# Two groups of every eight transposed wholly by blocks, with a sum, the routing and a product moved in the order

## The chip, the cores and the metric

The kernel runs on one core of one Trainium2 chip. The metric is the device time of one execution in microseconds, as the median of several runs. A profile of one execution shows the engines: TensorE (PE, with its weight loads as PEld), VectorE (DVE), ScalarE (ACT), GpSimd (POOL) and SyncE (SP), which issues DMAs.

## What is computed

A decoder layer on x of 16 sequences of 256 tokens with 256 channels, all in float32: three blocks, each followed by a layer norm over the residual.

```
x = layernorm(x + attn(x));  x = layernorm(x + xattn(x, ctx, frac));  x = layernorm(x + ffn(x))

attn:   scores = q k^T (k, v from weights, 4 heads of 64);  p = relu(scores)^2;  residual + p v
xattn:  16 heads of 16;  logits = Q K^T * scale
        D = clip(frac_k - frac_q, -0.2, 0.2)
        probs = softmax(gamma * logits + delta * (ap_h * max(D,0) + an_h * min(D,0)))
        out = (probs V) Wo^T + bo
ffn:    top1 = argmax(gate(x));  base = x wi^T + wi_b
        inter = relu(base + lora_B[top1] lora_A[top1] x);  out = inter wo^T + wo_b
```

## The kernel before

The first block (attn) comes first, in a loop over eight blocks of 512 rows. The change does not touch it. After it runs one loop over `n = 0 ... 65`, which holds the cross attention and nearly all of the ffn. The order of all instructions on every engine's queue is the order in which this loop writes them; there is no scheduler behind it.

**Groups.** One step of the loop is one group: four heads of one sequence, and there are 4 x 16 = 64 groups. In step n the names `now`, `nxt`, `last` and `older` are the groups n, n + 1, n - 1 and n - 2. For one group:

- `negative` (L642, GpSimd) writes the negative part of the bias into a tile `neg` of which there are three; `positive(g)` (L654, ScalarE) writes the positive part into PSUM bank g.
- `logits` (L664, PE, 32 small matmuls) adds the products into the four banks.
- `maxima` (L682, VectorE, eight instructions with one accumulator read each) adds bank and `neg`, writes the result over `neg`, and keeps the maximum of each row.
- Then the probabilities have to be transposed, so that keys lie on partitions. In the way of PE, `subtract` (L733) takes the maximum off, `turned(g)` (L743) transposes four 128x128 tiles per head into PSUM, and `exps(g)` (L750, ScalarE) takes the exponential on the way to `pT`.
- From group 14 to 61 a group is *direct*: heads 0 and 1 go by blocks instead. `exp_rows` (L696, ScalarE) takes the exponential in rows, `blocks` (L707, VectorE) transposes 32x32 blocks into a tile of its own (`z` for even groups, the tile `kT`, free by then, for odd ones) and writes it to DRAM (L712); `fetch` (L724) reads it back with four DMAs into the right rows of `pT`. Heads 2 and 3 keep the way through PE.
- `attend` (L764, PE) multiplies `pT` with the values into a bank `ps_v`; `keep` (L777) copies it out, every second group.

**Parts.** From n = 15 on, eight steps carry one block of 512 rows through the ffn; `part` is (n - 15) % 8, and there are six such cycles in the loop (cycle 31 to 38 is the third). Part 0 transposes the rows (L857), part 1 forms the gates (L872), part 2 and 3 are the `halved` steps: in part 2 `route` (L887 to L909) picks the expert, `turn_um` (L919) transposes the result, and in both `inner` (L945) computes four of the eight tiles of hidden units into the same four PSUM banks that the logits use, `lora` (L958) adds the low-rank part, and ScalarE and VectorE write relu of it to `hT` (L967, L971). Parts 4 to 7 form the last product, one quarter of the rows each: `finish(j)` is `outer` (L978, PE) and `add` (L991, VectorE: sum with the rows, then statistics). Parts 5 and 7 put it into a `ps_v` bank, so that `attend` of two groups comes one step later, together (`apart`). In part 3 the block before it is scaled and sent out (`done.ready`, L208 to L215 and L1006).

**The PSUM tiles** `ps_b` are used in a ring of three (`tile_b`), by transposes and products alike. SyncE's queue is in order: an issue that waits holds those behind it. The DMAs of the loop on it are those named, the fetch and write of values and sums (`gather`, `regroup`, `invert`, `spread`, L574 to L600), the loads of the next sequence (L444, L448) and the output.

**What stood in a whole cycle's order.** In the two halved steps `turned` and `exps` of the last group's heads 2 and 3 came directly after the maxima and ahead of `inner`; in all other direct steps they came at the end of the step. `blocks` of a group was written in its own step, except in parts 0 and 1, where it was written after the maxima of the next step (`later`). Its fetch came at the start of the next step, or at the end of it for `later`.

Of the kernel before, what the change touches and what calls it, by code (L numbers as in the profile page):

```python
# [9 lines left out]
FP = mybir.dt.float32  # L10
AF = mybir.ActivationFunctionType
ALU = mybir.AluOpType
# [10 lines left out]
def tile_decoder_layer(ctx: ExitStack, tc: tile.TileContext, a: dict, out: bass.AP):  # L23
# [403 lines left out]
    if True:  # L427
# [199 lines left out]
        class Group:  # L627
            def __init__(self, batch, og):
                self.batch = batch
                self.o, self.i = divmod(og, 2)  # L630
                self.direct = DIRECT <= 4 * batch.b + og < 4 * B - 2
# [43 lines left out]
            def maxima(self):  # L675
# [3 lines left out]
                for g in range(4):  # L679
                    minus = self.direct and g < 2  # L680
# [12 lines left out]
            def exp_rows(self, g):  # L693

                for j in range(2):
                    nc.scalar.activation(  # L696
                        self.t[:, g, j, :], self.t[:, g, j, :], AF.Exp,
                        bias=self.mx[:, g, j : j + 1], scale=-1.0,
                    )

            def blocks(self):

                if self.i:
                    self.z = kT.rearrange("p n (c h q) -> p n c h q", c=2, q=32)
                else:
                    self.z = pm.tile([P, 4, 2, 4, 32], FP, tag="z", bufs=1, name="z")
                nc.vector.transpose(  # L707
                    self.z.rearrange("p n c h q -> p h c n q"),
                    self.t[:, 0:2].rearrange("p g j (c n k) -> p (g j) c n k", c=2, k=32),
                )  # L710
                self.away = drams.tile([P, 4, 4 * P // 2], FP, tag="blocks", name="away_z")
                nc.sync.dma_start(  # L712
                    out=self.away, in_=self.z.rearrange("p n c h q -> p n (c h q)")
                )

            def room(self):
# [3 lines left out]
                self.pD = self.pT[:, 0:2].rearrange("p g (a c h q) -> p (g a) c h q", a=2, c=2, q=64)  # L720

            def fetch(self):
                for n in range(4):
                    nc.sync.dma_start(  # L724
                        out=self.pT[32 * n : 32 * n + 32, 0:2].rearrange("k g (a e) -> k (g a) e", a=2),
                        in_=self.away[:, n].rearrange("(r k) e -> k r e", k=32),
                    )

            def subtract(self, halves):
                for g, eng in ((2, nc.gpsimd),) if self.direct else zip((0, 2), halves):  # L730
# [21 lines left out]
            def attend(self):  # L752
# [4 lines left out]
                for k in range(2):  # L757
                    for g in range(4):
                        rhs = self.pT[:, g, k * S : (k + 1) * S]
                        to = batch.av[32 * g : 32 * g + 32, self.i * S : (self.i + 1) * S]  # L760
                        if self.direct and g < 2:
                            rhs = self.pD[:, :, k, g, :].rearrange("p r (j q) -> p j r q", j=2)
# [20 lines left out]
        MADE, DIRECT = 5, 14  # L783
# [649 lines left out]
```

## Time and profile before

| | us |
|---|---|
| median of 3 runs | 887.77 (887.74 to 887.83) |
| the profiled execution | 887.49 |
| its span in the profile | 885.7 |
| VectorE: maxima L682, 512 instructions of 420 ns | 181.5 |
| PE: transposes L743, 640 | 87.1 |
| PE: last product L978, 512 | 115.6 |
| VectorE: block transposes L707, 48 of 1.24 us | 59.6 |
| ScalarE: exponentials in rows L696, 192 of 498 ns | 81.3 |
| ScalarE: pT from PSUM L750, 160 of 590 ns | 87.4 |
| GpSimd: subtractions L733, 65 of 1.91 us | 124.0 |

In the page's first part each engine has its busy time, its share of the span, and its number of instructions. The granted TensorE clock is at 9 of 10 or more in all forty slices of the span. A line of a timeline gives the start in the span, the time until the last of the instructions it merges had ended, the engine, the source line, and how many there are; in square brackets stands the time for which the engine was idle before it and what ended that. In a view of waits the three numbers are the total, how often, and the longest. A line such as "ps_v<-pT,vaug" reads: written tile, then the tiles read.

### The profile page before, as it was taken

The numbers are of one execution on the slowest core, as the hardware profiler recorded it, in microseconds if no ns is written. First come the engines' busy times: TensorE is split into PE (matmuls) and PEld (weight loads), VectorE is DVE, ScalarE is ACT, GpSimd is POOL, SyncE is SP. The second block draws the span as 40 slices with busy tenths as digits, with TensorE's granted clock in tenths as the row PEclk, the third lists the DMA queues.
The fourth block names the chain that finished last, engine by engine and source line by source line (L and its number), as shares of the span: only waits on it lengthen the run. The fifth ranks groups of instructions, "written<-read, shape, count | busy, mean of one in ns | idle before, by whom it ended". The sixth has DMA issues, their size and how long they took to land.

```text
span 885.7 us, 20853 instructions
## 1 busy us (share of the span) xinstructions
PE 862.4 (97%) x7708; PEld 513.1 (58%) x7708; DVE 693.3 (78%) x1975; ACT 577.0 (65%) x1012; POOL 466.6 (53%) x455
## 2 busy tenths in 40 slices
PE   8999999999999999999999999999999999999997
PEld 4334444444456776567547656754765675576655
DVE  6878899889779898769778877877887787777444
ACT  5766777777788788647747765774875577475111
POOL 1100223322479898656828765883976678374010
PEclk9999999999999999999999999999999999999999
DMA  5501101010001333454454536445453644642001
GB/s 139 159 1 43 54 24 44 31 49 1 8 8 48 99 98 110 139 162 149 158 155 150 158 129 184 151 155 168 138 164 133 193 151 135 181 149 102 28 7 41
DMA packets 70373, 92.94 MB, mean 105 GB/s; under 512 B 13824, under 2 KB 55296, under 8 KB 70272
## 3 DMA queue, kind: packets, MB, share of 16 engines
q1 hardware_dynamic: 69696, 91.35, 33.2%
q8 instruction: 61, 1.00, 0.5%
q14 instruction: 40, 0.33, 0.1%
q10 hardware_dynamic: 576, 0.26, 0.1%
HBM read 50.43 MB, written 39.58 MB: 102 GB/s over the span
## 4 chain that ended last, share of the span: by engine, by line
PE 44%; DVE 11%; issue 2%; POOL 1%; ACT 1%; DMA 0%; ACTq 0%; POOLq 0%; DVEq 0%
PE ps_l L945 9%; PE ps_b L978 6%; PE ps_l L664 5%; PE ps_v L764 5%; PE ps_b L743 4%; DVE neg L682 3%; PE ps_b L614 3%; PE ps_v L978 3%; PE ps_b L477 2%; PE ps_l L958 2%; DVE z L707 1%; PE ps_b L503 1%; PE ps_b L532 1%; POOL neg L733 1%; DVE dpos L547 1%
## 5 line engine op out<-in xcount | busy, mean ns | idle before, releaser
L682 DVE CUSTOM_DVE_ANT_0 neg<-ps_l,neg 128x256 f32<-128x256 f32 x512 | 181.5, 420 | 41.4 <-PE ps_l L664 38.3
L642 POOL TENSOR_SCALAR neg<-dneg,aneg,delta 128x512 f32<-128x512 f32 x252 | 198.9, 804 | 20.9 <-PE ps_b L743 10.0
L654 ACT ACTIVATE ps_l<-dpos,apos_d 128x512 f32<-128x512 f32 x256 | 172.2, 688 | 49.9 <-DVE mx L682 30.9
L354 DVE TENSOR_TENSOR pr<-pr 128x1024 f32<-128x1024 f32 x128 | 153.8, 1243 | 30.2 <-ACT pr L353 29.8
L733 POOL TENSOR_TENSOR neg<-neg,mx 128x1024 f32<-128x1024 f32 x65 | 124.0, 1909 | 85.4 <-DVE mx L682 84.3
L353 ACT ACTIVATE pr<-ps_a 128x1024 f32<-128x1024 f32 x128 | 125.0, 1026 | 53.0 <-PE ps_a L345 52.7
L345 PE MATMUL ps_a<-xnT,kT 64*64 64x512 f32 x1024 | 124.6, 593 | 1.0 <-ACT xnT L330 0.4
L364 PE MATMUL ps_v<-pr,vv 64*64 64x512 f32 x1024 | 122.7, 589 | 0.0
L945 PE MATMUL ps_l<-xt,wi 128*128 128x512 f32 x248 | 111.7, 596 | 0.2
L750 ACT ACTIVATE pT<-ps_b 128x512 f32<-128x512 f32 x160 | 87.4, 590 | 32.4 <-PE ps_b L743 30.9
L743 PE MATMUL ps_b<-ident,neg 128*128 128x128 f32 x640 | 87.1, 277 | 3.4 <-ACT pT L750 2.3
L743 PEld LDWEIGHTS ps_b<-ident,neg 128*128 128x128 f32 x640 | 71.5, 141 | 24.0 <-issue 6.2
L364 PEld LDWEIGHTS ps_v<-pr,vv 64*64 64x64 f32 x1024 | 45.0, 133 | 64.5 <-issue 54.6
L379 POOL TENSOR_TENSOR xt<-xt,half 128x512 f32<-128x512 f32 x15 | 19.1, 1274 | 119.8 <-ACT half L378 119.8
L419 POOL TENSOR_TENSOR hid<-hid,bo 128x256 f32<-128x256 f32 x32 | 43.6, 1366 | 71.8 <-ACT hid L251 71.8
L696 ACT ACTIVATE neg<-neg,mx 128x256 f32<-128x256 f32 x192 | 81.3, 498 | 0.0
L764 PE MATMUL ps_v<-pT,vaug 128*32 128x256 f32 x1024 | 74.3, 385 | 7.2 <-DVE x L991 6.0
L664 PE MATMUL ps_l<-kM,qT 32*64 32x256 f32 x2048 | 79.8, 388 | 0.0
L345 PEld LDWEIGHTS ps_a<-xnT,kT 64*64 64x64 f32 x1024 | 41.9, 133 | 65.3 <-issue 52.5
L945 PEld LDWEIGHTS ps_l<-xt,wi 128*128 128x128 f32 x248 | 45.6, 191 | 49.4 <-issue 44.6
L978 PE MATMUL ps_b<-wof,hT 128*128 128x256 f32 x304 | 68.4, 380 | 0.0
L524 POOL TENSOR_SCALAR kM<-keys,of_head 128x512 f32<-128x512 f32 x22 | 38.7, 1760 | 48.4 <-DVE keys L513 48.4
(137 smaller groups left out, 1183.3 us busy)
## 6 DMA issues: line engine op xcount, KB each, us to landing
pT<-away_z SPq DMA_DIRECT2D x192, 128.0 KB
away_z<-z SPq DMA_DIRECT2D x24, 512.0 KB
away_z<-kT SPq DMA_DIRECT2D x24, 512.0 KB
away_v<-raw SPq DMA_DIRECT2D x16, 512.0 KB
cT<-in_ctxT SPq DMA_DIRECT2D x16, 256.0 KB
v<-away_v SPq DMA_DIRECT2D x32, 128.0 KB
invs<-rows SPq DMA_DIRECT2D x16, 256.0 KB
x<-in_x SPq DMA_DIRECT2D x7, 512.0 KB
```

Source lines behind the costliest of these rows:

```text
L345: nc.tensor.matmul(sc[64 * k : 64 * k + 64, h, :], lhsT=kT[64 * h : 64 * h + 64, q, hf * P + 64 * k : hf * P + 64 * k + 64], rhs=self.xnT[ ...
L353: nc.scalar.activation(pr, sc, AF.Relu)
L354: nc.vector.tensor_tensor(pr, pr, pr, ALU.mult)
L364: nc.tensor.matmul(self.acc[k][64 * h : 64 * h + 64, :], lhsT=vv[64 * k : 64 * k + 64, hf, 64 * q : 64 * q + 64], rhs=pr[64 * k : 64 * k + ...
L642: nc.gpsimd.tensor_scalar(self.neg[:, g], self.batch.dneg, aneg[:, h : h + 1], delta, ALU.mult, ALU.mult,)
L654: nc.scalar.activation(banks[g], self.batch.dpos.rearrange("p j k -> p (j k)"), AF.Copy, scale=apos_d[:, h : h + 1],)
L664: nc.tensor.matmul(banks[g][64 * h : 64 * h + 64, j * S : (j + 1) * S], lhsT=self.batch.qT[rows, self.o, j * P + 64 * h : j * P + 64 * h + ...
L682: nc.vector.tensor_tensor_reduce(out=self.t[:, g, j, :], in0=banks[g][:, j * S : (j + 1) * S], in1=self.neg[:, g, j, :], scale=-1.0 if min ...
L733: eng.tensor_tensor(rows, rows, top.to_broadcast([P, 4, S]), ALU.subtract)
L743: nc.tensor.transpose(ps[:, k * S + j * P : k * S + (j + 1) * P], self.t[:, g, j, k * P : (k + 1) * P], ident,)
L945: nc.tensor.matmul(self.banks[g], lhsT=wi[:, c, f * P : (f + 1) * P], rhs=self.xT[:, c, :], start=(c == 0), stop=False,)
L978: nc.tensor.matmul(ps[:, 0:C], lhsT=self.hT[f][:, j * P : (j + 1) * P], rhs=wof[:, f, :], start=(f == 0), stop=(f == FC - 1),)
```

## The change

- A direct group now has a number of `pairs`: 2 where `(n - 15) % 8` is 2 or 3, that is in groups 17, 18, 25, 26, 33, 34, 41, 42, 49, 50, 57 and 58, and 1 in the other direct groups. With two pairs all four heads go by blocks: eight exponentials in rows instead of four, two block transposes instead of one (the first into `z`, the second into `kT`), two writes of 512 KB, and four fetches of 256 KB instead of 128 KB. No subtraction, no `turned` and no `exps` is left for such a group. For every direct group the scratch in DRAM gets a dimension for the pair, so that of a whole group a write goes in rows of 1 KB, not 4 KB, and a fetch in rows of 2 KB, not 1 KB.
- In the halved steps `turned` and `exps` of the last group no longer stand ahead of `inner`; where the last group has one pair (part 2) they stand at the end of the step, as in the other direct steps.
- `later` now holds in part 2 too: the blocks of group 33 are written in step 34, after its maxima, and its fetch directly behind them. For all groups with `later` the fetch moves from the end of that step to directly behind the blocks.
- `route` moves ahead of the blocks of the last group in part 2.
- The first `finish` moves to the start of part 4, ahead of the logits. In parts 5 to 7 `finish` moves ahead of `blocks`.
- In part 3 the scaling of the older block's rows (`done.ready`) moves from VectorE to GpSimd; its three Newton steps stay on VectorE.

```diff
@@ Group @@
-                self.direct = DIRECT <= 4 * batch.b + og < 4 * B - 2
+                n = 4 * batch.b + og
+                self.direct = DIRECT <= n < 4 * B - 2
+                self.pairs = 0
+                if self.direct:
+                    self.pairs = 2 if n > DIRECT and (n - DIRECT - 1) % 8 in WHOLE else 1
...
+                self.away = drams.tile(
+                    [P, 4, self.pairs, 2 * P], FP, tag=f"blocks{self.pairs}", name="away_z"
                 )
+                for m in range(self.pairs):
+                    if m or self.pairs == 1 and self.i:
+                        z = kT.rearrange("p n (c h q) -> p n c h q", c=2, q=32)
+                    else:
+                        z = pm.tile([P, 4, 2, 4, 32], FP, tag="z", bufs=1, name="z")
+                    nc.vector.transpose(
...
+                    nc.sync.dma_start(
+                        out=self.away[:, :, m], in_=z.rearrange("p n c h q -> p n (c h q)")
+                    )
...
-                for g, eng in ((2, nc.gpsimd),) if self.direct else zip((0, 2), halves):
+                for g, eng in ((2, nc.gpsimd),)[: 2 - self.pairs] if self.direct else zip((0, 2), halves):
...
-        MADE, DIRECT = 5, 14
+        MADE, DIRECT, WHOLE = 5, 14, (2, 3)
@@ the loop @@
+            if ff and part == 4:
+                ff.finish(0)
             if now:
                 now.logits()
...
                 now.maxima()
-                now.later = n >= FIRST and part in (0, 1)
+                now.later = n >= FIRST and part in (0, 1, 2)
+            if halved and part == 2:
+                ff.route()
             if last and last.direct and last.later:
                 last.blocks()
+                last.fetch()
...
             if halved:
-                for g in range(2, 4) if last.direct else range(2):
-                    last.turned(g)
-                    last.exps(g)
-                if part == 2:
-                    ff.route()
-                if now.direct:
-                    for g in range(2):
-                        now.exp_rows(g)
+                now.exp_rows()
                 now.subtract((nc.gpsimd, nc.vector))
-                if now.direct:
+                if not now.later:
                     now.blocks()
...
-                    done.ready(newton(done.mv, done.near, 4))
+                    done.ready(newton(done.mv, done.near, 4), eng=nc.gpsimd)
                 ff.inner(part - 2, range(0, 3))
...
+            if ff and part > 4:
+                ff.finish(part - 4, tile_v() if apart else None)
             if now and now.direct and not halved and not now.later:
                 now.blocks()
-            if ff and part >= 4:
-                ff.finish(part - 4, tile_v() if apart else None)
-            if last and (not last.direct or now and now.direct and not halved):
-                for g in range(2, 4):
+            if last and (not last.direct or now and now.direct):
+                for g in range(2 * max(last.pairs, 1), 4):
                     last.turned(g)
                     last.exps(g)
...
-            if last and last.direct and last.later:
-                last.fetch()
```

## The prediction

> **What bounds the kernel now.** I read the page first, then the waits of TensorE, then TensorE's timeline through one cycle of eight groups (31 to 38; the stage of group n begins with its logits, L664), and last VectorE, ScalarE and SyncE beside it.
>
> ```profile
> PE 862.4 (97%) x7708; PEld 513.1 (58%) x7708; DVE 693.3 (78%) x1975; ACT 577.0 (65%) x1012; POOL 466.6 (53%) x455
> ```
>
> PE is busy 97% of 885.7 us, so only what leaves PE's own sequence, or the few waits in it, can shorten the kernel. The waits (us in total, times, longest):
>
> ```profile
> PE ps_v L764 <- DVE x L991: 6.0, 6, 1.6
> PE ps_b L919 <- DVE um L909: 2.6, 5, 0.5
> ...
> PE ps_b L503 <- DVE x L991: 0.7, 1, 0.7
> ...
> PE ps_b L464 <- DVE x L991: 0.2, 1, 0.2
> ```
>
> The last products' sums (L991) hold PE for 6.0 + 0.7 + 0.2 = 6.9 us, the routing (L909) for 2.6. What stands around the transposes that go (start, us, instruction; idle time in brackets):
>
> ```profile
> 449.84 1.60 PE L664 MATMUL ps_l<-kM,qT 32*64 32x256 f32 x32
> 451.37 1.09 PE L743 MATMUL ps_b<-ident,neg 128*128 128x128 f32 x8
> 452.58 7.13 PE L945 MATMUL ps_l<-xt,wi 128*128 128x512 f32 x16
> ```
> ```profile
> 452.10 0.42 DVE L682 CUSTOM_DVE_ANT_0 neg<-ps_l,neg 128x256 f32<-128x256 f32 x1
> ```
>
> That is group 26, one of the new "whole" ones' stages. The inner product L945 overwrites the bank that VectorE's maxima still read: bank 0 needs its two maxima, the second from 452.10 to 452.52. L945 starts at 452.58, though L743 was through at 452.46. So the eight transposes already stand in the shadow of the maxima.
>
> ```profile
> 497.99 1.25 DVE L707 STREAM_TRANSPOSE z<-neg 128x1024 f32<-128x1024 f32 x1
> 499.16 0.38 DVE L991 TENSOR_TENSOR x<-x,ps_v 128x256 f32<-128x256 f32 x1
> ```
> ```profile
> 499.60 2.65 PE L764 MATMUL ps_v<-pT,vaug 128*32 128x256 f32 x32 [1.10 <-DVE x L991]
> ```
>
> Here the sum that frees the bank stands behind a block transpose on VectorE, and PE waits 1.10 us for it.
>
> **Part by part.** Whole are the stages of parts 2 and 3: 17, 18, 25, 26, ... 57, 58, twelve groups in six cycles. My clock is cycle 31 to 38 (33 and 34 whole).
>
> *Sums ahead of block transposes (parts 5 to 7).* The sum then starts 1.17 us earlier (499.16 - 497.99), or earlier still where the transpose itself waited for exponentials (before 786.63 VectorE idled 2.03 us). That exceeds the waits of 0.78 to 1.10; the one of 1.63 (788.23) goes too. Next late is ScalarE: it idles 0.84 us before the copies of L860 at 504.65, and the positives ahead of them follow VectorE, whose summed work is unchanged. So 0.26 of the 1.10 stays. The six: 0.89 + 0.84 + 0.79 + 0.78 + 0.78 + 1.63 = 5.7; with 0.67 and 0.16, **-6.5 us**. Ends: nothing, and -6.9.
>
> *Part 2 (group 33).* Group 32's eight transposes are not removed but put at the stage's end. At their old place PE gains nothing: maxima begin 1.3 us after the logits, L945 still starts about 515.3. Route ahead of z: um comes 1.17 us earlier, so L919's 0.53 us goes. At the end +0.95 us of transposes (479.21 to 480.17), but the logits of 34, which ran 1.53 us instead of 1.05 (527.73 to 529.26 in the chain that ended last) because ScalarE's positives came late, lose that 0.48. 0.95 - 0.53 - 0.48 = **-0.06, taken as 0**. Ends: -0.5 and +0.5 a cycle.
>
> *Part 3 (group 34).* Group 33's transposes go, and the wait for the maxima, about 1.06 us, takes their place: **0**. VectorE now does maxima of 34 (to 532.2), two transposes of 33 (1.24 each, to 534.7), then z of 34. z is one buffer, so this waits until z of 33 has been written away. SyncE writes at about 533.5; the trace has 549.62 to 552.38, 2.76 us, from such an issue until the fetch behind it goes, and SyncE's own waits for these writes are at most 3.4 us elsewhere, 3.7 with the 0.34 of the issue. So z of 34 starts at 536.3, kT of 34 at about 537.7, through at 539. The three Newton steps (0.9) follow, then the hidden units' eviction at 540 instead of 538.53. Queued behind it are keys, dpos, the positives of 35 and the first last product. That product now runs 541.3 to 544.75 ahead of the logits, and covers it: positives of 35 end near 543.
>
> The writes' rows change: 512 of 1 KB for 128 of 4 KB. The fetches move 1 KB rows today with the same engines; I take equal speed. Ends: none, and 1.5 us more per write, the whole transfer again by these rows (packets of about 1.6 us between issue and landing). SyncE sends the fetch of 33 at 537.8, done about 542; its values are needed at 545.8. It also stands ahead of output, rows and the fetch of 34 in SyncE's queue, with needs near 557.
>
> ScalarE trades two pT copies (1.08 together) for four more exponentials (1.7) in each whole stage, inside idle times of 4.48 (before 522.08) and 5.93 us (before 538.49): 0. GpSimd loses two subtractions (1.9 each) a cycle and, in the five cycles with an older output, gains four row scalings: 0.56 us each by L845's row, 2.2 us. VectorE loses 1.38 (534.75, four). A row against it: dpos (L547) took 0.69 us at 528.37 with GpSimd idle, but 1.72 us at 495.40 beside GpSimd's L733 and L524. If it came to that here, 1.04 us of VectorE per cycle, covered by the first last product: 0, ends 0 and +1.0.
>
> [...]
>
> *Part 4 (group 35).* PE before: 541.28 logits (1.53), values 1.0, L532 1.9, first last product 3.45, transposes 0.88, L464 0.5, next logits 550.54. After: product to 544.75, logits 1.05 to 545.8, values 546.8, L532 548.6, L464 549.1. But now little lies between logits and logits. The sum of row 0 (1.0 us) and the maxima of 35 start near 546.0 (543.04 before). ScalarE's positives end 3.65 us after the maxima start (543.04, 546.69 before): 549.65. So the logits of 36 end near 550.7, not 551.6: **-0.9 us**.
>
> *Given back in parts 5 and 6.* The chain maxima 35, positives, exponentials, block transpose takes 5.31 + 1.24 us (543.04, 548.35, 549.60): the maxima of 36 start at 552.5 instead of 551.82. ScalarE then does positives, four exponentials, qT, in three cycles (36, 44, 52) one more row of L251 (0.5), and only then pT of 35: 7.64 us after the maxima's start with that row, 7.1 without, so 560.1 or 559.6. PE, 0.9 early, reaches them near 559.1: in the trace 559.46 stood against about 559.8. PE gives back about 0.5 without the row, 1.0 with it. Net -0.4 in three cycles, +0.1 in three: **-0.9**.
>
> Sum: -6.5 + 0 + 0 - 0.9 = -7.4 us, on the profiled execution's 887.49 (span 885.7): 880.1. The median of the runs, 887.77, is 0.3 above that execution; I forecast **880.0 us**.
>
> **Rivals.**
>
> *All transposes pay.* 96 fewer: twelve times 0.95 = 11.4 us, with the sums' 6.5 about 869.5. For it: PE is full, and every part's shadow might be filled by work I think is bound. Against it: 452.52 against 452.58 above. Chance 0.12.
>
> *The second pair waits for the first (slower).* At VectorE's z of 34, the wait for z's write blocks everything behind it: hidden units, positives, sum of row 0. Price: every us by which the write lands after 536.3, less the cover, which is about 1.7 us (positives of 35 at 543 against logits at 544.75), in each of six cycles. It ends slower than before once it exceeds the 7.4 gained: 7.4 / 6 = 1.2, so from 2.9 us late, a landing 5.7 us after issue. At 7 us after issue it costs (4.2 - 1.7) x 6 = 15 us: 895. For it: rows of 1 KB, and DMA share of 0.81 in 533 to 541 already. Against: 2.76 us in the trace, none over 3.7. Chance 0.12.
>
> *Given back entirely.* As forecast, but the pT of 35 or 1.5 us more per write costs 0.9 to 1.3 us more a cycle, 5.4 to 7.8 in six: 886 to 888. Chance 0.10, of which 0.08 lie within 0.2%.
>
> *The reorder does less than it says:* if PE's waits for L991 remain because another semaphore ends them (POOL's subtraction at 503.15 ends with PE's L743 at 505.05), only part 4 is left: 886.6. Chance 0.03, within 0.2%.
>
> **Numbers.** Forecast (875 to 885) 0.63; all pay 0.12; slower 0.12; given back 0.10; less than it says 0.03. A measurement of this kernel can tell about 0.2% (1.8 us). Faster 0.63 + 0.12 + 0.02 = 0.77; same 0.08 + 0.03 = 0.11; slower 0.12. Range 869 to 887: it takes in all-pay and most of given-back and leaves out 0.12 above, plus some 0.05.
>
> **What would show it.** Waits of PE for L991 under 1 us in all; L919 without wait; L945 with about 1 us of new idle time in each stage of part 3, ended by the maxima (right), or none (then all pay). Logits of 36 with a short wait for ScalarE. pT, L750, ending PE's wait at the second set of values in part 6. VectorE's second z in a stage idle about 1.6 us, ended by a DMA; over 4 us there, and the forecast is wrong. PE busy near 850.

## The result and the profile after

The changed kernel takes **948.5 us** (median of 4 runs, 945.0 to 949.8) against 887.75 (887.17 to 887.83) on the same chip: the ratio is 1.068, with a 95% interval of 1.0649 to 1.0711. The forecast was 880.0, so even its sign was wrong. The profiled execution took 949.77 us, with a span of 947.8, 62.1 more than before.

The page's row of busy times first:

```profile
PE 862.7 (91%) x7612; PEld 509.0 (54%) x7612; DVE 696.9 (74%) x1967; ACT 585.1 (62%) x1036; POOL 465.8 (49%) x463
```

TensorE has 96 instructions fewer and is as busy as before (862.4). So the 62 us are idle time of TensorE. Its waits say for what (us in total, times, longest):

```profile
PE ps_v L779 <- DMA pT<-away_z: 56.9, 21, 6.7
PE ps_l L960 <- DVE mx L686: 9.7, 12, 1.0
PE ps_v L779 <- ACT pT L765: 3.0, 6, 0.6
...
PE ps_b L477 <- ACT xT L471: 2.3, 4, 1.3
...
PE ps_b L934 <- DVE um L924: 0.3, 1, 0.3
```

The first row is new in its size: the value products (L779, L764 before) wait for the fetch of the turned blocks, 56.9 us where it was 0.5. The second is the wait for the maxima, 12 times some 0.8 us. The waits for the last products' sums (6.9 us before) and for the routing (2.6) are gone or nearly so. The ledger of the span: +56.4 (fetch), +9.7 (maxima), +2.6 (pT of ScalarE), +2.3 (xT), -6.9 (sums), -2.3 (routing) make 61.8 of idle time; busy time moves by +0.3.

That 0.3 hides two things. The transposes that went are worth 13.0 us: their group was 87.1 us (640) and is 74.1 (544). And something else costs TensorE as much. One cycle of TensorE (start, us, instruction; idle time ahead of it in brackets):

```profile
630.34 1.04 PE L758 MATMUL ps_b<-ident,neg 128*128 128x128 f32 x8
631.30 1.12 PE L668 MATMUL ps_l<-kM,qT 32*64 32x256 f32 x32
633.44 7.13 PE L960 MATMUL ps_l<-xt,wi 128*128 128x512 f32 x16 [1.02 <-DVE mx L686]
...
644.38 4.23 PE L993 MATMUL ps_b<-wof,hT 128*128 128x256 f32 x16
648.54 1.20 PE L668 MATMUL ps_l<-kM,qT 32*64 32x256 f32 x32
652.09 1.07 PE L779 MATMUL ps_v<-pT,vaug 128*32 128x256 f32 x16 [2.35 <-DMA pT<-away_z]
...
664.05 1.07 PE L779 MATMUL ps_v<-pT,vaug 128*32 128x256 f32 x16
671.40 1.94 PE L779 MATMUL ps_v<-pT,vaug 128*32 128x256 f32 x16 [6.28 <-DMA pT<-away_z]
673.27 3.78 PE L614 MATMUL ps_b<-wo,oT 128*128 128x256 f32 x8
```

Two waits for a fetch in one cycle, 2.35 and 6.28 us. Behind the long one the eight matmuls of L614 take 3.78 us; in the kernel with the orders alone (below) the same eight take 1.99, from 655.31. Busy times by stretch show why (window, its length, busy time and instructions of each engine, granted clock, DMA share, which can pass 1 in this view, GB/s):

```profile
659.00:664.00 5.00, 5.00 (x55) 4.00 (x53) 3.46 (x14) 5.00 (x11) 5.00 (x6) 1.00 1.09 202
664.00:670.00 6.00, 1.12 (x24) 0.42 (x16) 3.21 (x17) 5.77 (x12) 5.33 (x8) 0.79 0.59 186
670.00:678.00 8.00, 6.60 (x28) 4.48 (x29) 1.60 (x3) 0.14 (x1) 2.48 (x2) 0.52 0.63 202
```

After the wait the granted clock is 0.52. Over the whole span it is 0.971 (0.999 before). So each long wait is paid twice, as idle time and as slow work after it; by the ledger the second payment is 13.3 us (0.3 + 13.0).

SyncE in the same cycle (L722 writes blocks away, L739 fetches them, L585 is the values' read):

```profile
635.67 1.14 SPq L585 DMA_DIRECT2D v<-away_v  x2
636.91 0.57 SPq L722 DMA_DIRECT2D away_z<-z  x1
637.76 0.55 SPq L722 DMA_DIRECT2D away_z<-kT  x1
644.22 1.74 SPq L739 DMA_DIRECT2D pT<-away_z  x4
646.06 0.53 SPq L722 DMA_DIRECT2D away_z<-z  x1
646.69 0.58 SPq L722 DMA_DIRECT2D away_z<-kT  x1
...
654.38 2.81 SPq L739 DMA_DIRECT2D pT<-away_z  x4
...
658.93 0.43 SPq L722 DMA_DIRECT2D away_z<-kT  x1
667.01 1.75 SPq L739 DMA_DIRECT2D pT<-away_z  x4
```

The three fetches are those of a first whole group, a second whole group and the group behind them. Read them with TensorE's rows. The first goes 7.3 us after its first write (644.22 - 636.91) and lets TensorE start at 652.09, 7.9 us later. The writes of the second group wait behind it in the queue (its z is through on VectorE at 644.09, the write is issued at 646.06, behind the 1.74 us of the fetch's issues), so the second fetch goes at 654.38. The write of the third group, which has one pair, is issued at 658.93, behind that fetch and the loads of the next sequence. By the transfers' own records, the fetch's packets of 2 KB run from 655.3 (with those of one load among them until 664.1), the loads' packets of 1 KB from 661.2 to 665.2, and the write's 128 packets of 4 KB only from 663.3 to 666.5. Its fetch goes at 667.01, and TensorE waits until 671.40.

VectorE in the same cycle:

```profile
635.37 1.24 DVE L716 STREAM_TRANSPOSE z<-neg 128x1024 f32<-128x1024 f32 x1
636.53 1.20 DVE L716 STREAM_TRANSPOSE kT<-neg 128x1024 f32<-128x1024 f32 x1
642.84 1.25 DVE L716 STREAM_TRANSPOSE z<-neg 128x1024 f32<-128x1024 f32 x1 [5.11 <-DMA away_z<-z]
...
645.80 2.06 DVE L986 TENSOR_SCALAR hT<-ps_l,wib 128x512 f32<-128x512 f32 x3
```

This is the wait that the prediction priced: the write of the first z lands 5.9 us after its issue (636.91 to 642.84), not 2.76, and the second z stands 5.11 us idle, not 1.6. It looks like the culprit. The experiments show that it is not.

### The profile page after: what moved, and what is told of

Its sections match the earlier page's. It is cut to its first block, busy times and chain, and to the rows that moved or that the text cites. A ratio compares the mean times of both kernels' runs of the same rounds, so it can differ in the third digit from the quotient of the medians.

```text
span 947.8 us, 20630 instructions
## 1 busy us (share of the span) xinstructions
PE 862.7 (91%) x7612; PEld 509.0 (54%) x7612; DVE 696.9 (74%) x1967; ACT 585.1 (62%) x1036; POOL 465.8 (49%) x463
## 4 chain that ended last, share of the span: by engine, by line
PE 61%; DMA 18%; DVE 9%; ACT 5%; SPq 3%; issue 3%; ACTq 0%; POOL 0%; DVEq 0%; POOLq 0%
PE ps_a L345 12%; PE ps_v L364 12%; PE ps_l L960 8%; DMA away_z<-kT 8%; DMA pT<-away_z 7%; PE ps_b L993 5%; PE ps_v L779 5%; PE ps_b L614 4%; PE ps_b L758 3%; SPq L739 3%; PE ps_l L668 3%; ACT ps_l L658 2%; DVE neg L686 2%; DMA away_z<-z 2%; PE ps_b L477 2%
## 5 line engine op out<-in xcount | busy, mean ns | idle before, releaser
L779 PE MATMUL ps_v<-pT,vaug 128*32 128x256 f32 x1024 | 79.7, 408 | 59.9 <-DMA pT<-away_z 56.9
L765 ACT ACTIVATE pT<-ps_b 128x512 f32<-128x512 f32 x136 | 74.4, 589 | 70.2 <-PE ps_b L758 69.6
L748 POOL TENSOR_TENSOR neg<-neg,mx 128x1024 f32<-128x1024 f32 x53 | 101.2, 1911 | 30.2 <-DVE mx L686 26.1
L701 ACT ACTIVATE neg<-neg,mx 128x256 f32<-128x256 f32 x240 | 100.6, 496 | 6.2 <-DVE mx L686 6.2
L779 PEld LDWEIGHTS ps_v<-pT,vaug 128*32 128x32 f32 x1024 | 31.0, 113 | 107.5 <-issue 77.6
L758 PE MATMUL ps_b<-ident,neg 128*128 128x128 f32 x544 | 74.1, 276 | 2.9 <-ACT pT L765 2.3
L668 PE MATMUL ps_l<-kM,qT 32*64 32x256 f32 x2048 | 74.8, 387 | 0.0
L758 PEld LDWEIGHTS ps_b<-ident,neg 128*128 128x128 f32 x544 | 61.3, 141 | 18.8 <-ACT pT L765 4.9
```

The source lines that it names most:

```text
L668: nc.tensor.matmul(banks[g][64 * h : 64 * h + 64, j * S : (j + 1) * S], lhsT=self.batch.qT[rows, self.o, j * P + 64 * h : j * P + 64 * h + ...
L758: nc.tensor.transpose(ps[:, k * S + j * P : k * S + (j + 1) * P], self.t[:, g, j, k * P : (k + 1) * P], ident,)
L779: nc.tensor.matmul(to, lhsT=batch.va[:, k, self.head(g), :], rhs=rhs, start=(k == 0), stop=(k == 1),)
```

## The experiments

Theory **Q** (queue): whole groups send twice the bytes through SyncE's one queue, in transfers that are slow for their shape, and all fetches behind come late. Rival **V**: VectorE's wait for z holds what is queued behind it. Rival **O**: the new orders cost by themselves, whole groups or not.

### The orders without whole groups, and their parts

All orders of the change, no whole group (against the changed kernel):

```diff
-        MADE, DIRECT, WHOLE = 5, 14, (2, 3)
+        MADE, DIRECT, WHOLE = 5, 14, ()
```

> The changed kernel with no whole group: every direct group has one pair, all moves in the order stay. Theory Q (the time is lost in the transfers of the whole groups, which land late on the one queue): PE's waits for pT read back fall from 56.9 us to under 3, and the sums' 6.5 us is gained, less about 0.5 us a cycle for eight transposes back at the end of part 3: 880 to 884 us. Theory R (the moved order itself, the first last product ahead of the logits and the blocks of part 2 a step later, makes the transfers late): above 900.

Measured: 916.4 us, 1.0324 [1.0293, 1.0356]. The orders cost 28.6 us with no whole group at all (theory R of the expectation, rival O here); the prediction had them at a gain. TensorE's waits:

```profile
PE ps_v L779 <- DMA pT<-away_z: 10.4, 7, 3.6
PE ps_l L960 <- DVE mx L686: 10.0, 12, 1.0
PE ps_b L477 <- ACT xT L471: 6.3, 5, 1.5
PE ps_b L934 <- DVE um L924: 3.1, 6, 0.5
PE ps_v L779 <- ACT pT L765: 2.9, 6, 0.6
...
PE ps_b L464 <- DVE vaug L540: 2.5, 5, 0.5
```

The waits for the sums are gone here too, and five others stand in their place. The next three kernels divide them. First, the kernel before with only the last products and sums ahead of the block transposes:

```diff
+            if ff and part >= 4:
+                ff.finish(part - 4, tile_v() if apart else None)
             if now and now.direct and not halved and not now.later:
                 now.blocks()
-            if ff and part >= 4:
-                ff.finish(part - 4, tile_v() if apart else None)
```

> The kernel before, with one edit: the last products and their sums ahead of the group's block transposes in parts 4 to 7. By the prediction's first step PE's waits for L991 fall from 6.9 us to under 0.5 and the time by 6.5: 881 us. If those waits were ended by something else: 886 to 888.

Measured: 894.9 us, 1.0084 [1.0067, 1.0101]: slower, by 7.1 us, where I had counted -6.5. The execution in the profile was the quickest of the four, 890.66, so its waits account for only 3 us of this:

```profile
PE ps_v L764 <- DMA pT<-away_z: 8.0, 7, 2.5
PE ps_v L764 <- ACT pT L750: 3.0, 6, 0.6
...
PE ps_v L764 <- DVE x L991: 0.6, 1, 0.6
```

The wait for the sums fell from 6.9 to 0.6 as forecast. But the transpose now stands behind the sum, its write goes later (652.98 in place of 652.50 in one cycle) and so does its fetch (656.46 in place of 655.44); the value products, which had 0.5 us of waits for it, now have 8.0, and for ScalarE's pT 3.0. The order took the wait from the sums and gave it to the blocks, with more on top.

The second, the kernel before with only the first last product ahead of the logits of part 4:

```diff
+            if ff and part == 4:
+                ff.finish(0)
             if now:
                 now.logits()
...
-            if ff and part >= 4:
+            if ff and part > 4:
                 ff.finish(part - 4, tile_v() if apart else None)
```

> The kernel before, with only the first last product and its sums put ahead of part 4's logits. The orders as a whole cost 28.6 us; the orders of parts 0 to 3 with the late blocks cost 6.4 (894.2) and the sums ahead of the blocks 7.1 (894.9), which leaves 15. Theory A (the terms add): it costs this 15 by itself: 900 to 905, with waits of the queries' products for xT and of the value products for vaug of about 8 us, since the 3.6 us of products no longer stand between part 4's copies and what reads them. Theory B (the orders hurt each other): 886 to 892.

Measured: 898.1 us, 1.0122 [1.0107, 1.0138]: +10.2, between the two expectations. The place of the loss is plain in TensorE's rows:

```profile
627.45 1.99 PE L532 MATMUL ps_b<-wv,cT 128*128 128x256 f32 x8
629.28 1.04 PE L743 MATMUL ps_b<-ident,neg 128*128 128x128 f32 x8
630.80 0.66 PE L464 MATMUL ps_b<-ident,hid 128*128 128x128 f32 x4 [0.49 <-DVE vaug L540]
631.39 1.12 PE L664 MATMUL ps_l<-kM,qT 32*64 32x256 f32 x32
633.95 1.99 PE L477 MATMUL ps_b<-xT,wq 128*128 128x256 f32 x8 [1.44 <-ACT xT L471]
```

In the kernel before, the 3.62 us of that product stood between L532 and L743, and while it ran the copies were made that the products of L464 and L477 now wait for. Now 0.49 + 1.44 us are open in each of five cycles: 8.8 us in the waits (2.5 + 6.3), most of the 10.2.

The third, the orders of parts 0 to 3 and the late blocks, with parts 4 to 7 as before (against the changed kernel):

```diff
-        MADE, DIRECT, WHOLE = 5, 14, (2, 3)
+        MADE, DIRECT, WHOLE = 5, 14, ()
...
-            if ff and part == 4:
-                ff.finish(0)
             if now:
                 now.logits()
...
-            if ff and part > 4:
-                ff.finish(part - 4, tile_v() if apart else None)
             if now and now.direct and not halved and not now.later:
                 now.blocks()
+            if ff and part >= 4:
+                ff.finish(part - 4, tile_v() if apart else None)
```

> The changed orders of parts 0 to 3 alone (turned and its exponentials at the end of the stage, routing ahead, fetch right behind the late blocks, part 2's blocks late too, row scalings on GpSimd), no whole groups, and the last products and sums of parts 4 to 7 where they were before. The orders as a whole cost 28.6 us (916.4), the sums ahead by themselves 7.1 (894.9), which leaves 21.5 for the orders of parts 0 to 3 and for the first last product ahead of the logits. Theory M (middle): nearly all of it is the middle, 12 waits of about 1 us for the maxima that turned no longer covers, the routing beside GpSimd, and what xT's copies wait: 902 to 912. Theory F (first product ahead): the middle costs only the 12 us less the routing's gain: 888 to 897, with waits at the inner products of about 10 us all the same.

Measured: 894.2 us, 1.0074 [1.006, 1.0087]: +6.4, within expectation F (888 to 897). The wait for the maxima is there in full (9.8 us), since the eight transposes that lay in its shadow now stand at the stage's end. The routing gains nothing ahead of the transpose (3.1 us of waits for um, 2.6 before). In the kernel with all orders, VectorE and GpSimd show what stands beside it:

```profile
608.83 1.73 DVE L916 TENSOR_TENSOR hot<-lg,top 128x32 f32<-128x32 f32 x1
```
```profile
608.63 1.89 POOL L748 TENSOR_TENSOR neg<-neg,mx 128x1024 f32<-128x1024 f32 x1 [1.05 <-DVE lg L908]
```

A comparison of 32 elements takes 1.73 us, until GpSimd's subtraction ends at 610.52; the same line took 0.50 on the mean before, when a block transpose ran ahead of it. So the three parts are 6.4 + 7.1 + 10.2 = 23.7 of the 28.6; the other 4.9 come only where they stand together. Rival O holds for nearly half of the 60.8.

### One of the two whole groups

The same edit with one number, first part 2 and then part 3 whole (`WHOLE = (2,)`, `WHOLE = (3,)`):

> Whole groups in part 2 only (17, 25, ... 57). Q: the write of group 35's blocks stands behind a fetch of half the size, so the wait of some 6 us at the second values of part 6 goes, the one of 0.7 to 2.4 us in part 4 stays: 880 to 895 us. V (what costs is VectorE's wait for z inside one step): no second pair in the same step, so that wait goes as well; the time alone does not tell the two apart, the row of z does.

> Whole groups in part 3 only (18, 26, ... 58). Q: the fetch of 1 MB of group 34 still stands ahead of the write of group 35's blocks: PE waits 3 to 6 us a cycle at the second values of part 6, 900 to 930 us. V: z of 34 follows a single pair of 33, which for an odd group lies in the other buffer, so VectorE does not wait for z, and the time falls to 885 or less.

Measured: 914.3 and 924.3 us in one run each, with 24.6 and 17.2 us of waits for the fetched pT. Part 2 whole alone costs nothing over the orders, part 3 alone some 8 us, both together 32: what is dear is two whole groups one after the other. The first run still has 25.6 us of VectorE's waits for z, against what I expected (a single even group writes z too), and yet does not lose: a first sign against V. The second does not lack such a wait either, though its expectation had none. It moved to kT, into which the single pair ahead is transposed:

```profile
DVE kT L716 <- DMA away_z<-kT: 25.8, 6, 6.1
```
```profile
PE ps_b L993 <- DVE keys L513: 7.1, 4, 3.1
```

Behind that wait stand the keys on VectorE, and for the keys TensorE waits 7.1 us, in four cycles, ahead of the first last product: about the 8 us that this kernel loses. So the mechanism of V is real, with part 3 alone whole. In the changed kernel PE's list of waits has no row for the keys.

### The bytes and their shape

Half of each fetch left out, so that the second pair's values are those of the first (the output is then not the reference's):

```diff
-                        out=self.turned_in[32 * n : 32 * n + 32],
-                        in_=self.away[:, n].rearrange("(r k) m e -> k r (m e)", k=32),
+                        out=self.turned_in[32 * n : 32 * n + 32, :, 0 : 2 * P],
+                        in_=self.away[:, n, 0].rearrange("(r k) e -> k r e", k=32),
...
```

> The changed kernel, which fetches only the first pair of a whole group (512 KB instead of 1 MB) and uses it for all four heads: it leaves out the second pair's values, all writes stay. If the fetches' bytes set the lateness: waits for pT under 15 us, no half clock, 895 to 905 us. If the writes and VectorE's wait for z set it: waits above 35 us and above 925 us.

Measured: 913.1 us (one run), between the two expectations and nearer to the first; the waits for pT are 17.5, those of VectorE for z 24.9, as long as ever. So 35 us hang on the size of the fetch (its rows are halved too, to 1 KB), and VectorE's wait stays while they go. Then all bytes, but in one transfer over 128 partitions in place of four over 32 (the keys then lie in another order than the values' rows, so the output is not the reference's):

```diff
-                for n in range(4):
-                    nc.sync.dma_start(
-                        out=self.turned_in[32 * n : 32 * n + 32],
-                        in_=self.away[:, n].rearrange("(r k) m e -> k r (m e)", k=32),
-                    )
+                nc.sync.dma_start(
+                    out=self.turned_in,
+                    in_=self.away.rearrange("(r k) n m e -> (k n) r (m e)", k=32),
+                )
```

> The changed kernel, with every fetch as one DMA over all 128 partitions instead of four over 32 partitions each; same bytes and row lengths, but the keys come in another order than the values, so it leaves out the matching of the two. The 2 KB packets of the changed kernel take 150 to 170 ns in a fetch against 84 alone. If that is because 32 partitions take only half the rate: packets near 90 ns, the 1 MB through in 3 us instead of 5.3, SyncE 1.3 us shorter per fetch, waits for pT under 25 us, 905 to 920 us. If the rate is that of the DRAM side or of the queue: packets stay above 140 ns and the time above 935.

Measured: 912.3 us (one run), as good as half the bytes, and with 24.2 us of VectorE's waits for z it is 4 us below the orders alone. Waits of TensorE:

```profile
PE ps_v L778 <- DMA pT<-away_z: 15.4, 10, 3.2
PE ps_l L959 <- DVE mx L686: 10.0, 12, 1.0
PE ps_b L477 <- ACT xT L471: 6.4, 5, 1.5
```

By the transfers' own records between 450 and 840 us, a packet of 2 KB takes 146 ns (median) in the changed kernel and 84 here. The packets of a whole fetch of 1 MB run for 5.8 us there (median of ten fetches) and 3.9 us here, and the last ends 6.7 us after the issue there and 5.2 here; of a fetch of 512 KB in the kernel before they run for 2.6 us, and the last ends 3.6 us after the issue. So the whole fetches differ by 146 / 84 = 1.7 in the time of a packet and by 5.8 / 3.9 = 1.5 in their length. The 32 partitions alone do not account for it: in the fetches of 512 KB, to 32 partitions each as well, a packet of 1 KB takes 46 ns in the kernel before and in the changed one. Whether the rows of 2 KB matter beside the 32 partitions was not tested.

Two more touch the queue's order and the values' read. The fetch of a second whole group put behind the write of the group after it:

```diff
                 last.room()
-                if not last.later:
+                if not last.later and last.pairs < 2:
                     last.fetch()
...
             if now and now.direct and not halved and not now.later:
                 now.blocks()
+            if last and last.direct and not last.later and last.pairs == 2:
+                last.fetch()
```

> The changed kernel; the fetch of the group of part 3 (34), needed two steps later, stands behind the write of group 35's blocks on SyncE's queue instead of ahead of it. Theory Q1 (the 6 us waits in part 6 come from the write of 35 lying behind that 1 MB fetch): the write of 35 lands 6 us earlier, the two fetches then follow one another, PE's waits for pT fall from 56.9 us to about 35 and the time to 920 to 930 us. Theory Q2 (what counts is the sum of what the queue carries between two points, not its order): waits and time stay within 6 us of 948.

Measured: 944.6 us (one run), within 4 of the changed kernel, as Q2 expected: whichever goes first, the other is late. And the values read in one transfer whose slowest dimension is 8 in place of two with 4:

```diff
-                self.away_v = drams.tile([P, 2, 512], FP, tag="values", name="away_v")
+                self.away_v = drams.tile([2, P, 512], FP, tag="values", name="away_v")
...
-                rows = self.away_v.rearrange("(g d) i e -> i g d e", d=2 * HD)
-                for i in range(2):
-                    nc.sync.dma_start(
-                        out=self.v[64 * i : 64 * i + 64].rearrange("p o q -> p (o q)"),
-                        in_=rows[i, :, 0:HD],
-                    )
+                rows = self.away_v.rearrange("i (g d) e -> (i g) d e", d=2 * HD)
+                nc.sync.dma_start(
+                    out=self.v.rearrange("p o q -> p (o q)"), in_=rows[:, 0:HD]
+                )
```

> The changed kernel; the read of the values (regroup) as one DMA whose slowest dimension is 8, instead of two of 4, the scratch laid out for it. In the changed kernel those two keep 4 of the 16 engines busy for 2.7 us, and the first writes of the whole groups queue behind them there: VectorE waits 5.1 us for z. If that is the reason: VectorE's waits for z fall from 22.9 us to under 12, PE's wait in part 4 goes, and the time falls to 925 to 938 us. If the writes are slow by themselves (512 rows of 1 KB): no change beyond 4 us.

Measured: 939.5 us (one run), z's wait 18.8 in place of 22.9: a part, and less than expected. In the changed kernel the values' read runs from 637.0 to 641.0, not for 2.7 us but for 4.0, with 3.9 of its packets of 2 KB in flight on the mean (637.25 to 640.25), beside 12.5 of the writes' (638.25 to 640.25). After it the transfers run at a share of only 0.28 of all engines from 641 to 643.5, with the last packets of the first group's writes, 4.3 of them in flight on the mean (641.25 to 643). That fits the expectation's account; that they lie on the engines that the values' read kept busy is not shown, since the records do not name the engine.

### VectorE's wait, taken away

The rival that the prediction had named was never tested by those. So the second whole group's transposes go behind the hidden units:

```diff
                 now.subtract((nc.gpsimd, nc.vector))
-                if not now.later:
-                    now.blocks()
...
                 older.attend()
+                if not now.later:
+                    now.blocks()
```

> The changed kernel, with the block transposes of the second whole group (part 3) put behind the hidden units, so that VectorE no longer waits for the first group's write ahead of them. Theory V (VectorE's block is what costs, the rival that the prediction named): the 6 waits of 3.8 us behind its cover go, 948 becomes 925 to 932. Theory Q (the cost is that twice the bytes go out and come back through one queue of transfers): TensorE's waits for pT keep 50 us and more, 943 to 955.

Measured: 950.7 us, 1.0701 [1.0681, 1.0722]. VectorE's 22.9 us of waits for z's write are gone altogether, the first last product runs its 3.62 us without a stall (4.23 in the rows of the changed kernel above), and the kernel is no faster:

```profile
PE ps_v L779 <- DMA pT<-away_z: 57.7, 21, 8.4
PE ps_l L960 <- DVE mx L686: 10.0, 12, 1.0
```

So V falls for the changed kernel, as it does by the two kernels with the smaller or quicker fetch, which keep the wait and are 35 us faster. Of the 5 us in the cycle shown, 0.6 held TensorE at the last product; the rest was slack, and the fetch is what is late. With parts 4 to 7 in the old order as well (the last edit of the orders' third kernel above):

> The same, with the products and sums of parts 4 to 7 in the order of the kernel before. If the orders of parts 4 to 7 cost here what they cost alone (22 of 28.6 us): 920 to 928; if they are hidden behind the waits for pT anyway: 938 or more.

Measured: 937.4 us, 1.0562 [1.0533, 1.059]. The orders that cost 22 us alone cost 13 here; the rest, it seems, lies in the shadow of the fetches.

### Would it pay with cheap transfers?

One fetch over 128 partitions needs the keys in another order. Reading every fourth key in the block transpose gives it (shown here without the single fetch, which is as above; against the kernel before):

```diff
-                    self.t[:, 0:2].rearrange("p g j (c n k) -> p (g j) c n k", c=2, k=32),
+                    self.t[:, 0:2].rearrange("p g j (c k n) -> p (g j) c n k", c=2, k=32),
```

> The kernel before, with one fetch over 128 partitions in place of four over 32 (the block transposes read every fourth key, so that the keys land in their own order; output unchanged). If transfers are hidden in the kernel before (0.5 us of waits of TensorE for pT): 885.5 to 889, and packets at 84 to 100 ns in place of about 150. If the strided reading makes VectorE's transposes longer (1.2 us now) and it is late: 890 or more.

Measured: 908.9 us, 1.0246 [1.0224, 1.0269], much slower than the kernel before, for a reason of its own:

```profile
L707 DVE STREAM_TRANSPOSE z<-neg 128x1024 f32<-128x1024 f32 x24 | 49.5, 2064 | 12.9 <-ACT neg L696 12.6 <-issue 0.3
```

2064 ns (the mean, in ns, behind the busy time) where the same line took 1244 before: 48 transposes x 0.82 = 39 us more of VectorE, and TensorE's waits for the sums rise from 6.9 to 22.2 (15.7 + 3.6 + 2.9). The two kernels that combined this with the values' read by eight, on the changed kernel and on the kernel before with the sums ahead, carry the same burden:

> The changed kernel with one fetch over 128 partitions and the values read back by eight transfers' worth of engines, both with an unchanged output. If the two cheap transfers add up (one fetch alone 912.3, with 15.4 us of pT waits and 24.2 us of VectorE's wait for z; values alone took 4 us of z's wait): 905 to 911, waits for pT below 12. What then remains is what the orders cost. If the whole groups by themselves were worth their transposes, it would come below the orders alone (916.4) by about 13 us of TensorE: 903.

> The kernel before, with one fetch, the values read by eight, and the last products and sums of parts 4 to 7 ahead of the blocks. If the gain of the sums (6.9 to 0.6 us of waits at the last products) was eaten by later blocks' transfers (waits for pT 0.5 to 8.0): 881 to 886, waits for pT below 3. If it was eaten by the order on VectorE and ScalarE itself (waits for the exponentials 3.0 us, later maxima): 888 to 894.

Measured: 921.7 us (1.0373 [1.0353, 1.0392]) and 903.4 (1.0183 [1.0163, 1.0202]), outside all that was expected; they tell nothing of the transfers. So both once more with the transposes as they were. The keys' order is then not that of the values' rows, so the output is not the reference's. The first is the kernel before with the sums ahead, the second the changed one with parts 4 to 7 in the old order:

> As the kernel before with one fetch, values by eight and the sums ahead (903.4), but the block transposes read their rows as in the kernel before: the keys of the first pair then lie in another order than the values' rows, so the output is not the reference's; the work is the same. If the strided reading (2.07 us a transpose against 1.24) was all of that kernel's loss: 880 to 886, and waits for pT below 4. If late transfers ate the gain of the sums whatever their rate: 890 to 895.

> The whole groups with cheap transfers (one fetch over 128 partitions with the keys in another order than the values' rows, so that the output is not the reference's; values by eight) and with the products and sums of parts 4 to 7 in the order of the kernel before. One fetch alone gave 912.3 in the changed order. If the orders of parts 4 to 7 cost 22 us here too: 884 to 892, about the kernel before. If whole groups without their transfers' delay were worth the 13 us of TensorE that they free: below 882. If the waits for z and for the maxima keep their cost: 895 to 905.

Measured: 888.4 us, 1.0008 [0.9999, 1.0018], between its two expectations, and 903.1, 1.0183 [1.0157, 1.0209], within the third of its own. With cheap transfers the sums ahead lose nothing any more (894.9 to 888.4), and gain nothing: waits of 0.6 for the sums, 4.0 for fetches and 3.5 for ScalarE's pT add up to 8.1, where the kernel before has 6.9 + 0.5 + 0.4 = 7.8. And whole groups, with cheap transfers and without the orders of parts 4 to 7, are still 15 us slower than the kernel before, 9 of them beyond what the orders of parts 0 to 3 cost alone (894.2):

```profile
PE ps_l L960 <- DVE mx L687: 9.9, 12, 1.0
PE ps_v L779 <- DMA pT<-away_z: 9.5, 9, 2.8
PE ps_v L779 <- DVE x L1006: 5.4, 6, 1.5
```

The 13 us of transposes are paid back by 9.9 us of waits for the maxima that they used to cover, and the fetches' 9.5 come on top; TensorE's busy time is 864.8, not 849 (862.4 - 13.0), at a granted clock of 0.991. The last kernel adds the later transposes of part 3 to it:

> The same again with the cheap transfers (one fetch over 128 partitions, its keys in another order than the values' rows, so that the output is not the reference's; values by eight). Without the block on VectorE this was 903.1. If that block's 17.9 us of VectorE's waits held TensorE: 888 to 896. If not, 900 to 906, and what remains beside the kernel before is the 9.9 us of waits for the maxima and the transfers' 9.5.

Measured: 911.7 us, 1.0255 [1.0227, 1.0283], above both expectations and slower than 903.1: TensorE's waits for the fetch rise to 23.2 us, it seems since blocks written later make their fetch later. No version of the change that was run beats the kernel before.

## Why the prediction was wrong, point by point

**The steps that failed.** The prediction counted the orders at -7.4 us; alone they cost 28.6 (see the sums and part 4 below). The other 32.1 us (948.5 - 916.4) come from one step in part 3: a whole fetch was timed like a half one. "The fetches move 1 KB rows today with the same engines; I take equal speed" held roughly by the byte: the packets of 512 KB ran for 2.6 us, those of 1 MB for 5.8, where twice would be 5.2. But "SyncE sends the fetch of 33 at 537.8, done about 542" gives 1 MB only 4.2 us, where its last packet ended 6.7 us after the issue (3.6 for 512 KB) and TensorE could go on after 7.9. It also goes 7.3 us after its write and not 4.3, and all writes and fetches behind it move with it. Of these the prediction says only that the fetch of 33 "also stands ahead of output, rows and the fetch of 34 in SyncE's queue, with needs near 557": I had priced one transfer at its own need and never laid out the queue's next two. Half the bytes, or one transfer over 128 partitions, give back 35 and 36 us.

**Sums ahead, -6.5.** The waits did go (6.9 to 0.6, and to nothing in the changed kernel). "Next late is ScalarE" was incomplete: next late are the blocks' write and fetch (8.0 us of waits, 0.5 before), and alone the step costs 7.1.

**Part 2, taken as 0, with -0.53 for the routing.** In the changed kernel the wait for um shrank to 0.3; with the orders alone it stayed at 3.1. There the comparison took 1.73 us beside GpSimd's subtraction and not 0.50, which is as much as the 1.17 us gained; I had cited a like row for another instruction and set its cost to 0.

**Part 3, transposes for a wait of the maxima: 0.** Right in mechanism and size (1.02 us in each of the six stages of part 3, 0.33 to 0.65 in those of part 2, 9.7 in all; the eight transposes were 1.04).

**z's write, 2.76 us.** 5.9 were measured. The values' read ahead of it is a part of the reason (with a read by eight the waits fall from 22.9 to 18.8); the rest was not found. The rival built on this decided from 5.7 and so did come about as an event, and it named the right side. That was luck: the kernel without that wait is no faster, and the loss came by the fetches.

**Part 4, -0.9, and -0.9 net with what parts 5 and 6 give back.** Failed: the first last product covered the copies of values and xT. I moved it, worked out the logits of 36, and did not ask what had run beside it in its old place. +10.2.

**GpSimd's row scalings, 2.2 us.** 1.22 us each, 4.84 for four, not 0.56: the row that I took is another instruction. No wait of TensorE names it in the changed kernel.

**Half clock.** Not in the prediction at all; the profile of before shows no such stretch in the loop. By the ledger it is 13.3 us.

The signs that I had set were right as signs: waits for L991 (now L1006) under 1 us, new idle time of 1 us at the inner products, and "over 4 us there, and the forecast is wrong" for the second z (5.1). "PE busy near 850" was not (862.7), and the wait at the second set of values in part 6 was ended by the fetch, not by ScalarE's pT.

What stays open: the 4.9 us by which the orders together exceed their parts, how much of the half clock's cost would be left with short waits, and how the 1 MB would go in rows of 1 KB. An order of parts 0 to 3 that keeps the transposes in the maxima's shadow with whole groups was not tried.

## What to carry to other kernels

Work that is bound to go in a full engine's sequence may be the cover of another wait: before moving a product, list what finishes on other engines while it runs, since that becomes late by as much. When a change makes transfers larger, lay out the queue's whole cycle, each write and fetch with its issue and landing, and not just the one transfer at its own need; and a long visible stall is tested by taking it away, because the 5 us on VectorE were worth almost nothing. Count long waits on a full TensorE at more than their length: in the changed kernel the clock was at half for 6.8 or 10.2 us, in and after each wait of 5.5 to 6.7 us.

## What the runs showed of the hardware

- **Half clock at long waits.** In the changed kernel a stretch at half clock came with each of the six waits of 5.5 to 6.7 us. It began 2.3 to 4.0 us after the wait did, lasted 6.8 or 10.2 us, and held on for 3.6 to 6.3 us after the wait's end. It came with shorter waits too: 3.25 us in the changed kernel (3.4 us at half clock), 2.83 in the kernel with whole groups and cheap transfers (0.51 for the next 3.5 us), but not with the wait of 2.35 us shown above. After one wait of 3.62 us in the kernel with the orders alone the clock was 0.57 for the next 3.5 us, and the gates' products took 1.97 us where they take 1.08 in another cycle.
- **The shape of a transfer.** 1 MB in packets of 2 KB took 5.8 us in four transfers to 32 partitions each, at 140 to 162 ns a packet (median of a fetch), and 3.9 us in one to 128, at 84 ns; 1 KB packets to 32 partitions took 46 ns.
- **A strided read of VectorE.** Block transposes that read every fourth float took 2064 ns in place of 1244.
- **VectorE beside GpSimd.** A comparison of 32 elements a row took 1.73 us beside GpSimd's subtraction, 0.50 on the mean in the kernel before.
